# Rows spread by DMA instead of by transposes in a four-layer graph network

## The chip, the cores and the metric

The kernel runs on one core of a Trainium2 chip. The metric is the time of one execution on the device, in microseconds (us); lower is better. A core has five engines with a queue of instructions each: TensorE (PE, matmuls and transposes; its weight loads are listed as PEld), VectorE (DVE), ScalarE (ACT), GpSimd (POOL) and SyncE (SP, which here only issues DMAs). They wait for each other by semaphores.

## The reference

An array x of 32 samples, each 512 nodes by 256 features in float32, goes through four layers; every layer does `x = x + layer(relu(layernorm(x)))`. All layers are attention over the 512 nodes of a sample:

```
layer 0: 4 heads; softmax(q k^T / 8, masked by adj) v, then a product with wo
layer 1: o1 = relu(h mlp1 + b1)
         o2 = elu(gat(o1, no mask, W_fc)) + o1
         o3 = relu(o2 mlp2 + b2)
         relu(elu(gat(o3, adj, W_hand)) + o3)
         gat(o, mask, W): v = o W; e[i,j] = leaky_relu(f1[i] + f2[j]); elu(softmax_j(e) v)
layer 2: 4 heads of 64 features; e[i,j] = leaky_relu(src[i] + dst[j]), masked softmax over j,
         the weighted sum of the heads' features, then elu
layer 3: 8 heads of 32 features; as layer 2 with a prior of adj added to e, then a product with W_out
```

## The kernel before

One sample stays whole in on-chip memory: x as `xt` (128 partitions, 4 groups of nodes, 256 features), everything else in blocks of 128 x 512 floats (62 of them, one tag `block`) and in the eight PSUM banks (tag `bank`). Attention is computed transposed: a block `p[j]` holds 128 source nodes j by 512 target nodes i, so that it is the moving operand of the matmuls `av` directly, and its sum over j is wanted at the end. Softmax is never divided ahead of `av`; the sums of p are inverted and multiplied in afterwards.

The program is not issued in the order in which the source writes it. Every operation is recorded as a `Step` (through `_Recorder`, line 283, which is why all lines of the profile read L283). `Plan.order` then walks through all steps of all 32 samples and puts them in one order for each engine, by planned start and due time; `cost` gives it the assumed times, `STARTS`, `PACE` and `LAYERS` the earliest start of a sample and layer, `URGENT` shifts due times by the name of a tile and the layer, and `PERIOD` spaces the samples. Only the order and the buffers come out of the plan; on the chip the engines wait for semaphores. Two samples and more are in work at any time, so that PE has other samples' matmuls while one sample waits for ACT or DVE. In the steady part the pattern repeats for each two samples.

What the change touches:

- `on_all(name, cols)` (line 742) takes a column per group of nodes (128 x 4) and makes of it one row of 512 that stands on all 128 partitions. It transposes each column, repeated 128 times, on PE into a PSUM bank `pt` and copies that with ACT into a block. It is called four times per sample, in layer 1 only: `r1` in `first_gat` and `r2` in `second_gat` (factors of the target nodes, read by the four p1 or p2 blocks), and `rc` at the end of each `inverse_sums` (the inverse sums, by which `elu2` multiplies what `av` holds).
- `layer2(xt)` (line 914). `separable` computes two banks `av` (features by nodes) and a bank `sm` with the sums. `bars` copies the three to blocks `y3`. Then for each of the four groups of nodes 3 transposes bring them to node-major in a bank `pt`; DVE inverts 4 sums per node (`r4`), multiplies (`ue`), ACT takes the exponential, DVE adds to `xt` in two steps.
- `normalise(avs, sm)` (line 669), used before by layers 0 and 3 only: copies `sm` and `avs` to blocks (`sums`, `raw`), writes four rows of sums to DRAM (`s1`), reads them back spread over 128 partitions (`few`, 128 x 16), inverts them in one short DVE instruction, writes them to DRAM (`s2`) and reads them back repeated over the partitions of each head (`rc`); DVE multiplies (`oT`). All its DMAs are issued by SP.
- SP also loads the samples, stores the results, and spreads the rows `R` of layers 2 and 3 (`rd<-rT`, then 4 or 8 times `R<-rd`, 256 KB each). POOL issues the accumulating DMAs `p<-p`.

Of the kernel before, what the change touches and what calls it, by code (L numbers as in the profile page):

```python
# [15 lines left out]
AF = mybir.ActivationFunctionType  # L16
ALU = mybir.AluOpType
# [3 lines left out]
P = 128  # L21
N = 512
NT = N // P
D = 256
KD = D // P
# [7 lines left out]
H2, F2 = 4, 64  # L33
H3, F3 = 8, 32
# [7 lines left out]

PERIOD = 179.0
STARTS, PACE = (0.0, 0.0, 38.0, 159.0), 85.0
LAYERS = (0.0, 4.0, 2.0, 98.0)

URGENT = {
    "pt:0": 192, "mm:0": 49, "total:0": 70, "av:0": 68, "mm:1": 25, "total:1": -78, "rs1:1": 42, "av:1": -7,  # L50
    "p2:1": 104, "p3:2": -95, "total:2": -542, "ue:2": -396, "mv:3": -121, "mm:3": -158, "p3:3": -723,
    "av:3": -527, "total:3": -695,
}
BLOCKS, KEEP = 62, 2
KEEP_BANKS = 0
# [15 lines left out]
class Plan:  # L71
# [40 lines left out]
    def add(self, attribute, engine, op, args, kw):  # L112
        steps = self.samples[-1]
        out = kw["out"] if "out" in kw else args[0]
        busy, lasts = cost(engine, op, args, kw, out)
        step = self.joined or Step(engine, busy)
        if not step.calls:
# [31 lines left out]
    def release(self, sample, layer):  # L149

        first = len(STARTS) - 1
        return (STARTS[sample] if sample < first else STARTS[first] + (sample - first) * PACE) + LAYERS[layer]

# [165 lines left out]
def cost(engine, op, args, kw, out):  # L319

    src = next((kw[k] for k in ("in_", "in0") if k in kw), args[1] if len(args) > 1 else out)
    if not isinstance(src, bass.AP):
        src = out
    n = 1
    for _, k in (src if op in ("bn_stats", "reduce_max", "tensor_reduce") else out).ap[1:]:
        n *= k
    if engine == "PE":
        return (0.109 if op == "transpose" else max(0.224 if n < 3 else 0.0, n * 0.001676)), 0.165
    pointers = sum(isinstance(kw.get(k), bass.AP) for k in ("bias", "scale"))
    if op == "mul":  # L330
        pointers = 1
    if engine == "ACT":
        busy = 0.05 + 0.000832 * n + 0.093 * pointers + (0.0 if src.tensor.name.startswith(BANKS) else 0.043)
        return busy + (0.093 if "accum_out" in kw else 0.0), 0.12
    if engine == "DVE":
        if op == "reciprocal":
            return 0.06 + 0.0062 * n, 0.085
        if op == "tensor_scalar" and n == N:
            return 0.456, 0.075
        by_pointer = op == "scalar_tensor_tensor" and isinstance(args[2], bass.AP)  # L340
        return 0.066 + 0.00105 * n + (0.06 if by_pointer else 0.0), 0.085
    if engine == "POOL":
        if op == "dma_start":
            return 1.1, (5.2 if n == N else 8.0)
        return (1.0 if n < 16 else 0.683), 0.1
    size = 4
    for _, k in (out.ap if out.tensor.name.startswith(("few", "R", "rc", "x")) else src.ap):
        size *= k
    return 0.4, 3.4 + size / 190e3

# [2 lines left out]
def gnn_stack_kernel(ctx: ExitStack, tc: tile.TileContext, a: dict, out: bass.AP):  # L353
# [13 lines left out]
    x = a["x"]  # L367
# [4 lines left out]
    def T(ap, rearr, **kw):  # L372
        return ap.rearrange(rearr, **kw)
# [17 lines left out]
    ident = const.tile([P, P], F32, name="ident")  # L391
# [20 lines left out]
    r2 = w2[:, :, 3 * H2 + D :]  # L412
# [7 lines left out]
    def new_x():  # L420
        return first.tile([P, NT, D], F32, name="x", bufs=4)
# [4 lines left out]
    with prep_stack, tc.manual_schedule():  # L426

        adj = prep.tile([P, NT, N], I32, name="adj", bufs=1)
        av = T(a["adj"], "(t p) j -> p t j", p=P)
# [6 lines left out]
        row = prep.tile([1, 12 * P], F32, name="row", bufs=1)  # L436
# [146 lines left out]
    def pipelined(stack):  # L583

        big = stack.enter_context(tc.tile_pool(name="big", bufs=1))
        psum = stack.enter_context(tc.tile_pool(name="psum", bufs=8, space=PSUM))
        dram = stack.enter_context(tc.tile_pool(name="dram", bufs=6, space=bass.MemoryType.DRAM))
        q = Plan(nc, PERIOD)
        def block(name):

            return q.tile(big, [P, N], name, BLOCKS, keep=KEEP, tag="block")

        def blocks(name, n):
            return [block(name) for _ in range(n)]

        def bank(name):
            return q.tile(psum, [P, N], name, 8, keep=KEEP_BANKS, tag="bank")

        def small(name, *free):
            return q.tile(big, [P, *free], name, 4)  # L600
# [5 lines left out]
        def col(t):  # L606
            return slice(t * P, (t + 1) * P)
# [61 lines left out]
        def normalise(avs, sm):  # L669


            raws, sums = blocks("raw", len(avs)), block("sums")
            q.scalar.copy(sums, sm)
            for raw, av in zip(raws, avs):
                q.scalar.copy(raw, av)
            s1, s2 = q.tile(dram, [4, N], "s1", 8), q.tile(dram, [4, N], "s2", 8)
            q.sync.dma_start(s1, sums[0:P:32, :])
            few = small("few", 2, 4 * NT)
            c = 4 * N // P
            q.sync.dma_start(few[:, 0, :], T(s1, "h (p c) -> (h p) c", c=c))  # L680
            q.vector.reciprocal(few[:, 1, :], few[:, 0, :])
            q.sync.dma_start(T(s2, "h (p c) -> (h p) c", c=c), few[:, 1, :])
            dst = blocks("oT", len(avs))
            per = 4 // len(avs)
            for i, raw in enumerate(raws):
                rc = block("rc")
                for h in range(per):
                    f = P // per
                    q.sync.dma_start(rc[h * f : (h + 1) * f, :], s2[i * per + h : i * per + h + 1, :].to_broadcast([f, N]))
                q.vector.tensor_tensor(dst[i], raw, rc, op=ALU.mult)  # L690
            return dst
# [49 lines left out]

        def on_all(name, cols):

            pt, b = bank("pt"), block(name)
            for t in range(NT):
                q.tensor.transpose(pt[:, col(t)], cols[:, t : t + 1].to_broadcast([P, P]), ident)
            q.scalar.copy(b, pt)
            return b

        def largest(d):  # L750
# [9 lines left out]
        def inverse_sums(p):  # L760

            total = block("total")
            q.vector.tensor_tensor(total, p[0], p[1], op=ALU.add)
            q.vector.tensor_tensor(total, total, p[2], op=ALU.add)
            q.vector.tensor_tensor(total, total, p[3], op=ALU.add)
            sm, rs = bank("sm"), small("rs1", NT)
            for t in range(NT):
                q.tensor.transpose(sm[:, col(t)], total[:, col(t)], ident)
            q.vector.tensor_reduce(rs, T(sm, "p (t k) -> p t k", k=P), axis=AX.X, op=ALU.add)
            q.vector.reciprocal(rs, rs)  # L770
            rc = on_all("rc", rs)
            q.behind(sm)
            return rc
# [138 lines left out]
                bars(g, avs, sm)  # L912

        def layer2(xt):
            y = blocks("y3", 3)

            def bars(g, avs, sm):
                for b, ps in zip(y, avs + [sm]):
                    q.scalar.copy(b, ps)

            separable(xt, w2, H2, mask1T, bars)
            for t in range(NT):
                pt = bank("pt")
                for k in range(3):
                    q.tensor.transpose(pt[:, col(k)], y[k][:, col(t)], ident)
                r4 = small("r4", H2)
                q.vector.reciprocal(r4, pt[:, D : D + P : F3])
                ue = block("ue")
                u, eu = ue[:, :D], ue[:, D:]
                q.vector.tensor_tensor(  # L930
                    T(u, "p (h f) -> p h f", h=H2), T(pt[:, :D], "p (h f) -> p h f", h=H2),
                    r4[:, :, None].to_broadcast([P, H2, F2]), op=ALU.mult,
                )

                q.scalar.activation(eu, u, AF.Exp)
                q.vector.scalar_tensor_tensor(eu, eu, 1.0, xt[:, t, :], op0=ALU.min, op1=ALU.add)
                q.vector.scalar_tensor_tensor(xt[:, t, :], u, 0.0, eu, op0=ALU.max, op1=ALU.add)

        def layer3(xt):
            oT = []  # L940
# [84 lines left out]
        for i in range(B):  # L1025
            q.begin()
            q.sample, q.left = i, B - i
            xt = q.adopt(new_x() if i else x0, "x", 4)
            if i:
                q.sync.dma_start(xt, xv[i])  # L1030
            for q.layer, layer in enumerate((layer0, layer1, layer2, layer3)):
                layer(xt)
            q.sync.dma_start(ov[i], xt)
# [430 lines left out]
```

## Time and profile before

| | |
|---|---|
| time, median of 3 runs | 3960.52 us (3958.26 to 3962.6) |
| the profiled execution, its own time | 3964.65 us |
| its span in the profile | 3962.9 us |
| granted TensorE clock | 0.992 |
| busy: PE, DVE, ACT, POOL | 98%, 84%, 71%, 14% |
| DMA: bytes, share of the 16 engines | 292.57 MB; SP's queue 14.3%, POOL's 16.1% |

The table's shares are means over the span. In the views that follow, a group of instructions has its engine, the tiles it writes and reads (`out<-in`, buffer numbers left out), its shape and its count; then its busy time and the mean length of one. Matmuls overlap each other, so that a length is not what one costs: the distance from start to start is. A float32 matmul appears as two instructions, a transpose as one. A wait line reads: engine and tile, who released it, the sum in us, how often, the longest. In the timeline the first number is the start in us, the second the length of the group.

### The profile page before, as it was taken

How to read it: one execution, taken by the hardware profiler on the slowest of the kernel's cores; microseconds unless marked ns; L12 is line 12 of the kernel's file. 1: busy time of each engine (PE TensorE's matmuls, PEld its weight loads, DVE VectorE, ACT ScalarE, POOL GpSimd, SP SyncE). 2: the span in 40 equal slices, each digit the busy share in tenths (PEclk: the TensorE clock that was granted, in tenths of full speed). 3: DMA queues.
4: the chain of work that ended last, by engine and by line, in shares of the span. 5: the costliest groups of instructions: out<-in, count | busy, mean ns of one | idle time of the engine just before them, and what ended most of it. 6: DMA issues, size and time to landing. Idle time of an engine off the chain costs nothing.

```text
span 3962.9 us, 52558 instructions
## 1 busy us (share of the span) xinstructions
PE 3890.9 (98%) x17144; PEld 2149.1 (54%) x17144; DVE 3344.2 (84%) x7049; ACT 2805.9 (71%) x5968; POOL 566.4 (14%) x530
## 2 busy tenths in 40 slices
PE   8999999999999999999999999999999999999997
PEld 4655555555555555555555555555555555555552
DVE  6499898888888888988888988888888889888886
ACT  4577677766677766767766777666777667777665
POOL 0001111101111111111101111011111011111010
PEclk8999999999999999999999999999999999999998
DMA  3013333313233223333223333132332233332231
GB/s 101 21 37 81 72 82 84 92 44 92 57 89 92 71 65 76 76 84 84 67 63 78 76 88 88 49 89 59 86 92 73 63 76 76 84 83 69 71 77 50
DMA packets 217616, 292.57 MB, mean 74 GB/s; under 512 B 49915, under 2 KB 103422, under 8 KB 217334
## 3 DMA queue, kind: packets, MB, share of 16 engines
q0 software_dynamic: 68864, 111.18, 16.1%
q1 hardware_dynamic: 148196, 177.69, 14.3%
q8 instruction: 138, 2.26, 0.2%
q14 instruction: 144, 1.18, 0.1%
q10 hardware_dynamic: 274, 0.26, 0.0%
HBM read 158.79 MB, written 19.10 MB: 45 GB/s over the span
## 4 chain that ended last, share of the span: by engine, by line
PE 69%; DVE 17%; DMA 5%; ACT 4%; issue 2%; POOL 2%; SPq 1%; DVEq 0%; ACTq 0%; POOLq 0%
PE mm L283 33%; PE av L283 22%; PE sc L283 5%; PE pt L283 5%; DVE total L283 5%; DVE p L283 5%; DMA R<-rd 4%; PE sm L283 3%; ACT p L283 2%; POOL rs L283 2%; DVE o L283 1%; DVE ue L283 1%; DVE stats L283 1%; DVE x L283 1%; DVE y L283 1%
## 5 line engine op out<-in xcount | busy, mean ns | idle before, releaser
L283 ACT ACTIVATE p<-R,e 128x512 f32<-128x512 f32 x1536 | 993.4, 727 | 53.2 <-DMA R<-rd 52.3
L283 PE MATMUL av<-p,v 128*128 128x512 f32 (+1 forms) x2560 | 930.8, 596 | 4.5 <-DVE p L283 4.4
L283 DVE SCALAR_TENSOR_TENSOR p<-p,e,mask3T 128x512 f32<-128x512 f32 x1024 | 720.5, 749 | 8.1 <-ACT p L283 8.1
L283 POOL TENSOR_TENSOR rs<-ve,mhalf 128x4 f32<-128x4 f32 x128 | 202.5, 1582 | 2755.9 <-DVE ve L283 2634.4
L283 PEld LDWEIGHTS av<-p,v 128*128 128x128 f32 (+1 forms) x2560 | 348.2, 169 | 446.5 <-issue 357.2
L283 DVE TENSOR_TENSOR total<-total,p 128x512 f32<-128x512 f32 x872 | 572.6, 687 | 1.4
L283 PE MATMUL av<-p,vs 128*32 128x512 f32 (+1 forms) x3072 | 504.5, 598 | 5.6 <-DVE p L283 5.4
L283 PE MATMUL mm<-W_fc,o 128*128 128x256 f32 (+1 forms) x2048 | 468.4, 380 | 2.8 <-ACT o L283 2.8
L283 PEld LDWEIGHTS mm<-W_fc,o 128*128 128x128 f32 x2048 | 382.5, 190 | 85.3 <-issue 29.4
L283 POOL DMA_DIRECT2D p<-p x360 | 323.9, 1047 | 564.2 <-PE av L283 191.2
L283 DVE SCALAR_TENSOR_TENSOR p<-p,e,mask1T 128x512 f32<-128x512 f32 x512 | 350.7, 748 | 41.0 <-ACT p L283 40.4
L283 ACT ACTIVATE h<-x,ms,rs 128x256 f32<-128x256 f32 x512 | 280.1, 628 | 122.9 <-DVE ms L283 121.0
L283 DVE TENSOR_TENSOR p<-p,mask0T 128x512 f32<-128x512 f32 x512 | 328.5, 690 | 17.4 <-ACT p L283 17.2
L283 PEld LDWEIGHTS av<-p,vs 128*32 128x32 f32 (+1 forms) x3072 | 138.4, 118 | 342.2 <-issue 238.6
L283 DVE TENSOR_TENSOR total<-p,p 128x512 f32<-128x512 f32 x436 | 288.7, 687 | 0.0
L283 ACT ACTIVATE p<-sc 128x512 f32<-128x512 f32 x512 | 254.3, 679 | 7.8 <-PE sc L283 7.8
L283 PE MATMUL mm<-w,hT 128*128 128x272 f32 (+1 forms) x1024 | 254.4, 393 | 0.9 <-ACT hT L283 0.8
L283 PE MATMUL mm<-hT,mlp_w 128*128 128x512 f32 x512 | 237.6, 596 | 0.0
L283 PE MATMUL mm<-o,mlp_w 128*128 128x512 f32 x512 | 234.7, 596 | 1.3
L283 PE MATMUL sc<-qT,kT 64*128 64x512 f32 x1024 | 230.1, 599 | 0.0
L283 PEld LDWEIGHTS mm<-w,hT 128*128 128x128 f32 x1024 | 190.6, 191 | 61.0 <-issue 15.3
L283 ACT COPY rc<-pt 128x512 f32<-128x512 f32 x64 | 37.4, 585 | 246.8 <-PE pt L283 246.7
(183 smaller groups left out, 5457.5 us busy)
## 6 DMA issues: line engine op xcount, KB each, us to landing
R<-rd SPq DMA_DIRECT2D x384, 256.0 KB
p<-p POOLq DMA_DIRECT2D x360, 256.0 KB, 5.3
x<-in_x_dram SPq DMA_DIRECT2D x32, 512.0 KB
x<-boa POOLq DMA_DIRECT2D x32, 512.0 KB, 5.5
rc<-s SPq DMA_DIRECT2D x128, 128.0 KB
out_dram<-x SPq DMA_DIRECT2D x32, 512.0 KB
rc<-s SPq DMA_DIRECT2D x248, 64.0 KB
s<-sums SPq DMA_DIRECT2D x94, 8.0 KB
```

What stands on the lines that cost most here:

```text
L283: getattr(getattr(self.nc, attribute), op)(*args, **kw)
```

## The change

`on_all` transposes all four columns at once (128 x 4 to 4 x 128), copies the 4 rows to a tile `turned`, lets SP write them to a row in DRAM and lets SP read that row back onto all 128 partitions. `turned` shares its four buffers with `rT` of layers 2 and 3. Layer 2 calls `normalise` ahead of its transposes, so that 2 blocks instead of 3 are transposed, two groups of nodes at a time in one bank, and the elementwise work runs on 512 columns at once from PSUM. The planner's constants are new, and `cost` counts a DMA into r1 and r2 by its destination.

```diff
-PERIOD = 179.0
-STARTS, PACE = (0.0, 0.0, 38.0, 159.0), 85.0
-LAYERS = (0.0, 4.0, 2.0, 98.0)
+PERIOD = 157.0
+STARTS, PACE = (0.0, 7.0, 65.0, 129.0), 95.0
+LAYERS = (0.0, 6.0, 0.0, 143.0)
 
 URGENT = {
-    "pt:0": 192, "mm:0": 49, "total:0": 70, "av:0": 68, "mm:1": 25, "total:1": -78, "rs1:1": 42, "av:1": -7,
-    "p2:1": 104, "p3:2": -95, "total:2": -542, "ue:2": -396, "mv:3": -121, "mm:3": -158, "p3:3": -723,
-    "av:3": -527, "total:3": -695,
+    "stats:0": 39, "mm:0": -259, "p0:0": -88, "oT:0": 727, "mv:1": 15, "pt:1": 831, "mx:1": -151,
+    "nd:1": -62, "r1:1": 187, "total:1": -9, "rc:1": -74, "av:1": -240, "p2:1": -39, "stats:2": -144,
+    "h:2": -284, "p3:2": -269, "av:2": -418, "stats:3": -14, "p3:3": -685, "total:3": -152, "gp:3": 41,
 }
...
-    for _, k in (out.ap if out.tensor.name.startswith(("few", "R", "rc", "x")) else src.ap):
+    for _, k in (out.ap if out.tensor.name.startswith(("few", "R", "r1", "r2", "rc", "x")) else src.ap):
...
         def on_all(name, cols):
 
-            pt, b = bank("pt"), block(name)
-            for t in range(NT):
-                q.tensor.transpose(pt[:, col(t)], cols[:, t : t + 1].to_broadcast([P, P]), ident)
-            q.scalar.copy(b, pt)
+            pt, few = bank("pt"), q.tile(big, [P, P], "turned", 4)
+            q.tensor.transpose(pt[:NT, :P], cols, ident)
+            q.scalar.copy(few[:NT, :], pt[:NT, :P])
+            row = q.tile(dram, [NT, P], "row", 8)
+            q.sync.dma_start(row, few[:NT, :])
+            b = block(name)
+            q.sync.dma_start(b, T(row, "t p -> (t p)")[None, :].to_broadcast([P, N]))
             return b
...
         def layer2(xt):
-            y = blocks("y3", 3)
+            y = []
 
             def bars(g, avs, sm):
-                for b, ps in zip(y, avs + [sm]):
-                    q.scalar.copy(b, ps)
+                y.extend(normalise(avs, sm))
 
             separable(xt, w2, H2, mask1T, bars)
-            for t in range(NT):
+            for t in range(0, NT, 2):
                 pt = bank("pt")
-                for k in range(3):
-                    q.tensor.transpose(pt[:, col(k)], y[k][:, col(t)], ident)
-                r4 = small("r4", H2)
-                q.vector.reciprocal(r4, pt[:, D : D + P : F3])
-                ue = block("ue")
-                u, eu = ue[:, :D], ue[:, D:]
-                q.vector.tensor_tensor(
-                    T(u, "p (h f) -> p h f", h=H2), T(pt[:, :D], "p (h f) -> p h f", h=H2),
-                    r4[:, :, None].to_broadcast([P, H2, F2]), op=ALU.mult,
-                )
-
-                q.scalar.activation(eu, u, AF.Exp)
-                q.vector.scalar_tensor_tensor(eu, eu, 1.0, xt[:, t, :], op0=ALU.min, op1=ALU.add)
-                q.vector.scalar_tensor_tensor(xt[:, t, :], u, 0.0, eu, op0=ALU.max, op1=ALU.add)
+                for i in range(2):
+                    for k in range(KD):
+                        q.tensor.transpose(pt[:, col(2 * i + k)], y[k][:, col(t + i)], ident)
+                u, xs, eu = T(pt, "p (t d) -> p t d", d=D), xt[:, t : t + 2, :], block("eu")
+
+                q.scalar.activation(eu, pt, AF.Exp)
+                eu = T(eu, "p (t d) -> p t d", d=D)
+                q.vector.scalar_tensor_tensor(eu, eu, 1.0, xs, op0=ALU.min, op1=ALU.add)
+                q.vector.scalar_tensor_tensor(xs, u, 0.0, eu, op0=ALU.max, op1=ALU.add)
```

## The prediction

> **What bounds the kernel now.** I read the engine shares on the page first, then the windows view for the stretch without head and tail, then the waits of PE in that stretch. On the page PE is busy for 98% of the span, and its row of tenths is 9 nearly from end to end, while DVE has holes:
>
> ```profile
> PE 3890.9 (98%) x17144; PEld 2149.1 (54%) x17144; DVE 3344.2 (84%) x7049; ACT 2805.9 (71%) x5968; POOL 566.4 (14%) x530
> ...
> PE   8999999999999999999999999999999999999997
> ...
> DVE  6499898888888888988888988888888889888886
> ...
> PE 69%; DVE 17%; DMA 5%; ACT 4%; issue 2%; POOL 2%; SPq 1%; DVEq 0%; ACTq 0%; POOLq 0%
> ```
>
> The windows view splits head, middle and tail (columns: length, busy us and instructions of PE, PEld, DVE, ACT and POOL, granted clock, DMA share, GB/s); the waits of PE in the middle follow:
>
> ```profile
> 0.00:250.00 250.00, 230.09 (x890) 127.14 (x891) 149.36 (x356) 130.40 (x259) 15.43 (x20) 0.95 0.18 50
> 250.00:3750.00 3500.00, 3483.38 (x15372) 1930.92 (x15371) 3031.81 (x6363) 2544.99 (x5438) 535.89 (x494) 1.00 0.32 76
> 3750.00:3963.00 213.00, 177.42 (x885) 91.08 (x883) 163.03 (x332) 130.51 (x274) 15.10 (x16) 0.91 0.24 66
> ```
>
> ```profile
> PE mm L283 <- ACT o L283: 8.4, 17, 1.9
> PE mm L283 <- ACT hT L283: 3.8, 14, 0.3
> PE av L283 <- DVE p L283: 2.8, 3, 1.3
> ```
>
> PE waits visibly for 15 us of 3500, at full clock. So PE is the bound: an instruction taken from PE shortens the kernel by the time until the next may start, and work on DVE, ACT or the DMA queues is free as long as no PE instruction waits for it. Busy time is no proof of this alone (ends of matmuls are modelled), so I also use spacing of starts. In the timeline, twelve transposes run like this, and the small row transposes of layer 1 alike:
>
> ```profile
> 1517.40 0.27 PE L283 MATMUL pt<-ident,mx 128*128 128x128 f32 x1
> 1517.60 1.06 PE L283 MATMUL sm<-p,ones 128*32 128x512 f32 x8
> ...
> 1531.52 1.53 PE L283 MATMUL pt<-ident,y 128*128 128x128 f32 x12
> ...
> 1543.40 0.62 PE L283 MATMUL pt<-ident,rs 128*128 128x128 f32 x4
> ```
>
> (1.53 - 0.27 of the last one's own length - 0.06 of the first's late start) / 11 = 0.11 us from start to start: that is the price of a transpose on PE, not the 0.27 that one lasts. The first pair shows another price: 0.20 us from the transpose to a matmul on 32 columns, so 0.09 us for the change from the full array to columns.
>
> **What the Trainium skill says.** "TensorE: Matmul & The Clock Gate", Part 4, gives about 275 ns for a 128x128 transpose inside a kernel; the trace agrees for the length (273 ns median), but in a burst only 109 ns of it stand on PE. "TensorEngine Tiling (Array Packing)", Key Properties, says that changing the tiling mode drains TensorE; the 0.09 us agree. "DMA: Bandwidth & Descriptors", Anatomy of one DMA, gives a fixed cost of about 2 us, mostly the receipt of the write, and says that semaphores are waited for on the issuing sequencer ahead of dispatch. The trace agrees: SP issues the read of a small row only once its write has landed, 1.83 us later:
>
> ```profile
> 1608.69 0.62 SPq L283 DMA_DIRECT2D rd<-rT  x1
> 1610.52 2.60 SPq L283 DMA_DIRECT2D R<-rd  x4
> ```
>
> **The change part by part.**
>
> *Work on PE.* on_all is called 4 times per sample (r1, rc, r2, rc): 4 transposes of 128x128 become one with 4 output rows. Layer 2 transposes 8 instead of 12 times per sample. Over 32 samples 512 + 384 = 896 go and 128 + 256 = 384 come, 512 fewer x 0.109 = 55.8 us. The narrow transpose has no row here; the nearest, of 16 columns (es), also takes 0.11 us to the next start; between 0.06 and 0.20 us each, 128 of them would move the sum by -6 to +12. The diff's new constants of the planner also reorder PE. In the order of the built programs the tiling mode changes 558 times before and 491 times after (the branch that isn't run counts alike in both): 67 x 0.093 = 6.2 us. Together 62 us of PE.
>
> *ACT.* Gone: 128 copies of r and rc (38.3 + 37.4 us) and 128 exps of ue (45.4). New: 128 copies of 4x128 (about 0.25 each, the rT row: 32) and 64 exps of 128x512 (about 0.63: 40). The 96 copies of y3 become 96 of raw and sums. 49 us less.
> *DVE.* Gone: r4, the product ue and its two additions (15.7 + 45.6 + 51.0 + 50.3 = 163 us). New: 64 products oT (0.69), 128 additions of 128x512 (0.69), 32 reciprocals few (0.24): 140. 23 us less. Neither is on the path, and both get lighter; I count nothing. The cover is PE's own work.
>
> *DMAs.* 128 x (one row written, one 256 KB broadcast), and for layer 2 32 x (3 small ones and 4 of 128 KB): 480 more issues on SP, at 0.3 to 0.65 us about 0.2 ms of its 3.9 ms, and 50 MB on 292.57 (+17%). The share of the DMA engines rises from 0.32 to about 0.37. SP's queue is in order: behind a row waiting for its transpose or its landing stand other samples' R loads, sums and rows; ACT (p) and DVE (oT) wait for these, and PE for p and oT.
>
> *The new latency.* A row used to take 4 transposes and a copy, about 1.3 us. Now: transpose 0.27, copy 0.25, write 1.83, broadcast 3 to 7 us (256 KB of p<-p lands in 5.3 by the page; I take 5.3), so 7.7. For r1 the DVE op follows (0.55): 8.2 to the first p. For r2 exp and mask (0.72 + 0.75): 9.1. For rc the chain of elu2 (0.69 + 3 x 0.65 + 2 x 0.69 = 4.0): 11.7 until o2. For layer 2 (sums 0.59, three hops of 1.8 to 2, reciprocal 0.24, issues 1.7, landing 2 to 5, product 0.69): 11 to 14. What must be weighed against this is how much PE work the order puts between. I added up the PE instructions of the built order with the spacings of the trace (0.43 us for 512 columns, 0.22 for 256, 0.11 for a transpose):
>
> r1 to the first av: 3.0 us before, 16.7 to 17.0 after. r2 to the first av: 3.0 and 9.4 before, 17.2 and 12.1 after (even and odd samples). rc to the first matmul on o2: 8.2 and 16.7 before, 18.8 and 17.5 after. Layer 2's sums to its transposes: 0.1 to 1.0 before, 19.9 after.
>
> So the new planner constants moved every consumer back further than the latency grew; 3 us remain at the tightest place (odd r2), 6 or more elsewhere. In the middle I take 0, between -14 (before, PE loses 0.9 us each second sample where layer 2's sm waits for DVE's total; this may go) and +25 (a broadcast lands 5 us late behind a burst of R loads in one of six rows, less than a quarter of it uncovered, plus waits at odd r2).
>
> *Head and tail.* The head's order differs a little (release times); I take its time as before. In the tail the cover is thinner: for sample 30 layer 2's sums have 5.6 us of PE work instead of the 11 needed, for sample 31 rc has 9.3 against about 11.7, and layer 2's first transposes follow layer 1's last without filler (3.5 us before). I take +6, between 0 and +15.
>
> *Sum.* 62 - 6 = 56 us less. The profiled execution took 3964.65 us (span 3962.9), 4.1 above the median of 3960.52. 3964.65 - 56 = 3908.7, on the scale of the median 3904.6: **3904**.
>
> **Rivals.**
> 1. *The broadcasts collide.* The DMAs come in bursts (4 or 8 R loads of 256 KB, then p<-p). For it: in the contended stretch at 1504.9 ACT waits 0.8 and then 1.7 us for R issued over 5 us earlier. Against: 12 to 20 us of cover. If PE loses 1.5 us per sample, 48 us, 3904 + 32 to 48 = 3936 to 3952. Chance 0.10.
> 2. *SP's queue becomes the pace* (slower). 160 new round trips block SP for about 2 us each, and a late one holds the next sample's, so cover is lost in chain. It decides once PE loses more than (56 + 8) / 160 = 0.4 us per round trip; at 0.7 us the time is 3904 + 112 = 4016, at 0.5 us 3984. For it: SP order of the changed program weaves rows of two samples with sums and R loads. Against: SP is idle before most issues now and what it waits for is mostly producers (945 us for rT in the queue's own waits). Chance 0.08.
> 3. *PE's saving is taken up by DVE*, at 0.87 of the middle, so that the transposes' place turns into waits for p or total: time between 3953 and 3968, no change. Against: DVE gets 23 us less. Chance 0.04.
> That the transposes do not go is excluded by the built order.
>
> **How the numbers follow.** Likeliest case 0.78, own range 3878 to 3938 (3904 with the bounds above: -14 middle, -6 tail, -6 narrow transposes, to +25 middle and +9 tail). Rivals 0.10, 0.08, 0.04. A measurement can tell 0.2% from no change, 8 us here: faster 0.88, same 0.04, slower 0.08. The range 3872 to 3942 takes in half of rival 1; out of it are rivals 2 and 3, the rest of 1 and a few hundredths below.
>
> **What would show it.** Right: about 16600 PE instructions, the rows pt<-ident,ew and pt<-ident,rs with 4 columns x64 each; PE still 97% or more and 0.99 in the middle; middle waits of PE under 40 us; total waits of SP changed, without effect. A longer tail by 5 to 10 us. Wrong: PE waits for p behind DMA r<-row, or for o behind DMA rc<-row, over 60 us in all; PE in the middle at 97% or less.

## The result and the profile after

The change made the kernel slower: 4030.45 us (median of 4 runs, 4027.66 to 4036.13) against 3959.39 for the kernel before on the same chip, a ratio of 1.0176 with a 95% interval of 1.0164 to 1.0189. That is 70 us more, where 56 less were predicted. The profiled execution took 4027.66 us, its span is 4025.9, so the profile stands 3 us under the median.

The same lines of the page as before (engines: busy us, share of the span, instructions; then PE's row of tenths and the shares of the chain that ended last):

```profile
PE 3845.7 (96%) x16632; PEld 2095.4 (52%) x16632; DVE 3323.7 (83%) x6761; ACT 2738.1 (68%) x5904; POOL 532.1 (13%) x530
...
PE   7999999999999999999999999999999999999977
...
PE 71%; ACT 11%; DMA 7%; DVE 6%; issue 2%; SPq 2%; POOL 0%; DVEq 0%; ACTq 0%; POOLq 0%
```

PE has its 512 instructions less. It is busy for 45 us less, and yet the span is 63 us longer: PE stands still (is not busy) for 4025.9 - 3845.7 = 180 us, against 3962.9 - 3890.9 = 72 before. The windows view says where (columns as before: length, busy us of PE, PEld, DVE, ACT, POOL, granted clock, DMA share, GB/s):

```profile
0.00:250.00 250.00, 228.72 (x852) 131.30 (x854) 128.81 (x319) 124.25 (x258) 15.54 (x21) 0.99 0.22 59
250.00:3750.00 3500.00, 3393.12 (x14753) 1849.97 (x14749) 2995.63 (x6054) 2455.55 (x5312) 497.75 (x491) 0.99 0.37 88
3750.00:4026.00 276.00, 223.90 (x1031) 114.16 (x1030) 199.31 (x390) 158.34 (x337) 18.78 (x18) 0.89 0.25 70
```

The head is nearly the old one (PE stands for 21 us, 20 before). In the middle PE stands for 107 us instead of 17, in the tail for 52 instead of 36. The largest waits of PE in the middle (us in total, times, longest):

```profile
PE mm L283 <- DVE oT L283: 42.9, 25, 2.6
PE pt L283 <- ACT h L283: 23.5, 25, 2.9
PE mm L283 <- ACT hT L283: 21.2, 42, 0.9
```

None of them is directly a wait for what the change gave a longer way. PE does not wait for p behind r or for o behind rc, and for layer 2's oT at its transposes only 5.5 us. It waits for oT, the normalised blocks of layers 0 and 3, whose code the change does not touch, and for h and hT, the layer norm at a layer's start. Before, these rows had 0, 0 and 3.8 us in the middle.

One such wait in full. The timeline of SP's queue shows the inverse sums of layer 0 for the second sample of a pair (start, us, tiles, how many). The rows s<-few at 1547.06 and rc<-s at 1549.68 belong to the chain ahead of it, layer 2's sums of another sample, and the rows with `row` to layer 1:

```profile
1545.62 0.52 SPq L283 DMA_DIRECT2D s<-sums  x1
1547.06 0.31 SPq L283 DMA_DIRECT2D s<-few  x1
1547.46 0.41 SPq L283 DMA_DIRECT2D few<-s  x1
1549.68 2.71 SPq L283 DMA_DIRECT2D rc<-s  x4
1554.18 0.33 SPq L283 DMA_DIRECT2D s<-few  x1
1555.54 0.47 SPq L283 DMA_DIRECT2D row<-turned  x1
1559.88 1.99 SPq L283 DMA_DIRECT2D rc<-s  x3
1562.06 1.93 SPq L283 DMA_DIRECT2D rc<-row  x1
1564.04 1.20 SPq L283 DMA_DIRECT2D rc<-s  x1
```

The chain that ended last and DVE's timeline continue it:

```profile
1562.12 1.86 SPq L283
1563.99 0.05 issue
1564.04 5.75 DMA rc<-s
```

```profile
1565.96 0.69 DVE L283 TENSOR_TENSOR oT<-raw,rc 128x512 f32<-128x512 f32 x1 [2.52 <-DMA p<-p]
1569.88 0.69 DVE L283 TENSOR_TENSOR oT<-raw,rc 128x512 f32<-128x512 f32 x1 [2.51 <-DMA rc<-s]
```

The sums leave at 1545.62 and the second product ends at 1570.57: 25 us. Three of the four broadcasts go out at 1559.88; the fourth stands in the queue behind layer 1's `rc<-row` and lands 5.75 us after its issue. PE has done all that stood between by 1568.1 and waits until 1570.6.

I followed every such chain of the middle in this way, from the issue of s<-sums to the end of the last product, by the order of instructions on SP and DVE. For layer 0 the two samples of a pair take 18.9 and 27.3 us before, and 19.7 and 24.3 after. So the chain is not longer on the whole. What changed is what it is set against: the PE work that the built order puts between sums and product was 19.1 and 35.2 us before, enough for both, and is 20.2 and 22.3 after, 2 us too little for the second. These waits are about half of the 42.9 us: the lines of the middle put 21.0 us to layer 0's matmuls (mm<-woT,oT) and 21.8 to layer 3's (mm<-L_WoT,oT).

### The profile page after: what moved, and what is told of

The parts are those of the page before. It is cut to its first block, busy times and chain, and to the rows that moved or that the text cites. A ratio compares the mean times of both kernels' runs of the same rounds, so it can differ in the third digit from the quotient of the medians.

```text
span 4025.9 us, 52303 instructions
## 1 busy us (share of the span) xinstructions
PE 3845.7 (96%) x16632; PEld 2095.4 (52%) x16632; DVE 3323.7 (83%) x6761; ACT 2738.1 (68%) x5904; POOL 532.1 (13%) x530
## 4 chain that ended last, share of the span: by engine, by line
PE 71%; ACT 11%; DMA 7%; DVE 6%; issue 2%; SPq 2%; POOL 0%; DVEq 0%; ACTq 0%; POOLq 0%
PE mm L283 40%; PE av L283 21%; ACT p L283 4%; DMA rc<-s 4%; PE pt L283 4%; PE sm L283 3%; PE sc L283 3%; DVE p L283 2%; ACT e L283 2%; ACT h L283 2%; SPq L283 2%; DMA s<-few 1%; DVE total L283 1%; DMA R<-rd 1%; ACT hT L283 1%
## 5 line engine op out<-in xcount | busy, mean ns | idle before, releaser
L283 DVE SCALAR_TENSOR_TENSOR p<-p,e,mask1T 128x512 f32<-128x512 f32 x512 | 363.0, 744 | 75.0 <-ACT p L283 73.3
L283 POOL TENSOR_TENSOR rs<-ve,mhalf 128x4 f32<-128x4 f32 x128 | 170.8, 1335 | 1908.1 <-DVE ve L283 1901.7
L283 PE MATMUL mm<-o,mlp_w 128*128 128x512 f32 x512 | 250.1, 611 | 2.0 <-DVE o L283 2.0
L283 ACT ACTIVATE e<-y 128x512 f32<-128x512 f32 x192 | 117.0, 625 | 188.2 <-DVE y L283 187.9
L283 ACT COPY v<-mm 128x512 f32<-128x512 f32 (+2 forms) x384 | 161.2, 444 | 116.0 <-PE mm L283 83.6
L283 ACT COPY raw<-av 128x512 f32<-128x512 f32 x190 | 109.2, 583 | 188.4 <-PE av L283 186.0
```

Source lines behind the costliest of these rows:

```text
L283: getattr(getattr(self.nc, attribute), op)(*args, **kw)
```

## The experiments

A ratio has a half-width (of its 95% interval) of about 0.0017 here, 7 us, so a difference of two runs is known to about 9 us; differences below are of ratios times 3960. The work of PE that an edit adds or removes is counted as in the prediction (0.109 us per transpose, 0.093 per change of tiling mode).

**Constants and code apart (four runs).** The diff changes code and the planner's constants (`PERIOD`, `STARTS`, `PACE`, `LAYERS`, `URGENT`) at once. e_ac_bc is the changed code with the old constants, e_bc_ac the old code with the new ones; e_onall_ac and e_l2_ac are the new constants with one half of the new code each.

```diff
 # e_ac_bc: code of after, constants of before;  e_bc_ac: the reverse
-PERIOD = 157.0
-STARTS, PACE = (0.0, 7.0, 65.0, 129.0), 95.0
-LAYERS = (0.0, 6.0, 0.0, 143.0)
+PERIOD = 179.0
+STARTS, PACE = (0.0, 0.0, 38.0, 159.0), 85.0
+LAYERS = (0.0, 4.0, 2.0, 98.0)
 ...
```

> The changed code (on_all by DMA, layer 2 by normalise) planned with the constants of the kernel before (PERIOD, STARTS, PACE, LAYERS, URGENT). Theory A, order: the new constants, which put two samples close together and leave more of both samples for the end, cost the time, and the code saves PE work as forecast: 3900 to 3940. Theory B, transfers: the new round trips make PE's operands late whatever the order: 4000 or more, as the old constants were made for short rows.

> The code of the kernel before, planned with the new constants. Theory A, order: it shows the new ramp, the new tail (39 us longer from the last transpose of a maximum to the end) and pairs of samples 64 and 13 us apart: 4010 to 4060, no faster than the changed kernel. Theory B, transfers: without the new DMAs the steady part loses its waits for oT: 3960 to 3985.

> Only on_all is changed (layer 2 as before), new constants. Theory A: 42 us of PE less than the old code under these constants, so about 40 below e_bc_ac. Theory B: 128 of the 160 new round trips are in it, so it is near the changed kernel, 4010 to 4040, and above e_bc_ac.

> Only layer 2 is changed (on_all by transposes as before), new constants. Theory A: 14 us of PE less than the old code, about 10 to 15 below e_bc_ac. Theory B: a fifth of the new round trips, so 3970 to 3990, between the old code under these constants and the changed kernel.

Measured: 4368.16 (ratio 1.1035, 1.1017 to 1.1053), 4318.26 (1.0904, 1.0885 to 1.0922), 4297.97 (1.0844, 1.0826 to 1.0862) and 4311.69 (1.0887, 1.0869 to 1.0905). All four are over 300 us slower than before, far more than was expected of any of them. So constants and code fit each other or don't, and the constants alone, with the code kept, move this kernel by 8 to 9% (4368.16 against 4030.45 for the changed code, 4318.26 against about 3962 for the old). An edit that changes the list of operations cannot be tried on this kernel without either keeping the order or fitting it anew; the other runs do the one or the other.

**Layer 1's rows within the changed order (e_pe, e_spare).** Both keep the order and plan of the changed kernel. In e_pe a row is made by four transposes and a copy again, and its DMAs are not issued. In e_spare they are issued at their old places, with the broadcast going into a tile in DRAM that nobody reads; so its queue and bytes are those of the change, its destination is not.

```diff
+            turn, copy, write, read = q.samples[-1][-4:]
+            turn.calls = [
+                ("tensor", "transpose", (pt[:, col(t)], cols[:, t : t + 1].to_broadcast([P, P]), ident), {}) for t in range(NT)
+            ]
+            copy.calls = [("scalar", "copy", (b, pt), {})]
+            write.calls, read.calls = [], []                # e_pe
             ...
+            write.calls = [("sync", "dma_start", (row, b[:NT, :P]), {})]        # e_spare
+            read.calls = [("sync", "dma_start", (spare, T(row, "t p -> (t p)")[None, :].to_broadcast([P, N])), {})]
```

> The changed kernel with its order and plan kept, only that layer 1's rows are made as before: four 128x128 transposes and one ACT copy straight into the block; the two DMAs of a row are not issued. PE gets 384 transposes more (3 of 0.109 us for each of 128 rows, 42 us). Theory A: the order stays and PE has 42 us more, so 4065 to 4080. Theory B: 42 us more of transposes, but the waits for oT go (30 to 40 us of wait and as much again at half rate behind it): 3965 to 4010, with PE's waits for DVE oT under 20 us.

> As e_pe (rows by four transposes and a copy, +42 us of PE), but the same two DMAs of each row are still issued at the same places of SyncE's queue: the row goes to DRAM and its broadcast of 256 KB goes into a spare DRAM tile that nobody reads. Nothing waits for the rows any more, but queue and DMA traffic are those of the change. Theory A: as e_pe, 4065 to 4080. Theory B: queue and traffic make oT late as in the changed kernel, so about 4070 as well, while e_pe lies 60 us or more below it. If e_pe and e_spare are both near 3990, what costs time is the wait of layer 1's own chain for its rows.

Measured: 4035.76 (1.0183, 1.0166 to 1.0200) and 4062.92 (1.0254, 1.0237 to 1.0271). PE's wait for oT in the middle, changed kernel 42.9 us, e_pe, then e_spare:

```profile
PE mm L283 <- DVE oT L283: 13.2, 19, 1.9
```

```profile
PE mm L283 <- DVE oT L283: 28.1, 26, 1.9
```

The second sample's layer-0 chain took 22.8 us in e_pe and 23.8 in e_spare, against 24.3. e_pe does 42 us more on PE than the changed kernel and is 3 us slower, so without the transfers the same work takes 39 us less. e_spare brings 28 of them back although nobody waits for its rows; the 11 that remain, little more than the error, are left for the wait for the rows. Neither theory had this: A expected e_pe at 4065 or more, B the whole loss in the transfers and e_pe at 4010 or less. It is about half: the transfers cost nearly what the transposes saved, PE's wait for layer 0's and layer 3's oT goes with them, and e_pe still stands 73 us above before.

**The place in the queue alone (e_pull).** SP's later broadcasts of a block are issued right behind its first, so that no `rc<-row` stands between as at 1562.

```diff
-        steps, at = self.order(), {}
+        steps, at = gathered(self, self.order()), {}
         ...
+        # gathered: on SP, outside layer 1, a later rc<-s moves up to the first one of its block
```

> The changed kernel, its order kept on every engine but SyncE: there the later rc<-s broadcast of a block is issued directly behind the block's first one, so that no broadcast rc<-row of layer 1 stands between the two in SyncE's queue. Theory A (the order that was written for the change sets the time: samples nearly in step with each other, a longer tail; SyncE's queue takes no part): within 8 us of the changed kernel, 4030. Theory B (the new row transfers on SyncE make layer 0's and layer 3's inverse sums late, PE waits for oT, and runs at half rate after each wait): PE's wait for DVE oT falls from 55 us to under 25, and with what follows each wait the time is 3960 to 3995. If only the transfers' landing is late and not the issue of the fourth broadcast, B also gives about 4025.

Measured: 4030.68 (1.0169, 1.0151 to 1.0186), no change. PE's wait for oT in the middle fell from 42.9 to 31.5 us, all of it layer 0's, whose chain is 1 us shorter (23.3), but the wait for h behind it rose from 23.5 to 31.8.

```profile
PE mm L283 <- DVE oT L283: 31.5, 25, 2.3
```

So the fourth broadcast's place, which the timeline shows so plainly, was worth nothing by itself, and an oT wait that goes is not time saved as long as another chain stands close behind.

**Layer 2's trip within the changed order (e_nol2, e_l2spare, e_none).** After the runs with fitted orders below, the trip of layer 2's sums was open. Again in the changed kernel's order: e_nol2 does not issue its seven transfers per sample and leaves out layer 2's division by the sums (the products take a constant), e_l2spare does the same but issues the transfers, with few<-s and rc<-s landing in spare DRAM tiles, and e_none is e_nol2 with e_pe's rows, so without any of the new transfers.

```diff
                 q.vector.tensor_tensor(dst[i], raw, rc, op=ALU.mult)
+                if q.layer == 2:
+                    q.samples[-1][-1].calls = [
+                        ("vector", "tensor_tensor", (dst[i], raw, eps[:, 0:1].to_broadcast([P, N])), dict(op=ALU.mult))
+                    ]
+            if q.layer == 2:
+                for step in q.samples[-1][-12:]:
+                    if step.engine == "SP":
+                        step.calls = []          # e_l2spare: few<-s and rc<-s go to spare DRAM tiles
 ...
```

> The changed kernel, its order and plan kept, but layer 2's seven transfers per sample are not issued: sums, inverse sums and their four broadcasts stay out, the reciprocal takes a constant, and both products of raw and rc take a constant in place of rc. That leaves layer 2's normalisation out. PE has the changed kernel's work, and layer 2's products wait for the raw blocks alone. If layer 2's trip through DRAM is what makes the changed code slow in every order so far (4000 to 4030) while layer 1's half alone went to 3936: 3960 to 3990. If its cost lies in the order and in what DVE and PE do, 4015 to 4030.

> As e_nol2, but the seven transfers are issued at their places of SyncE's queue and land in spare DRAM tiles that nobody reads; the products still take a constant. Traffic and queue are those of the change, the waits for the inverse sums are gone. If layer 2's cost is traffic and queue (layer 0's and layer 3's trips late behind it), within 10 us of the changed kernel, 4020 to 4040; if it is the wait for layer 2's own inverse sums, within 10 us of e_nol2.

> Both halves' transfers gone: the changed kernel's order, rows by four transposes and a copy (42 us more of PE), and layer 2 as in e_nol2, its normalisation left out. PE has then 20 us less than before the change. If the transfers together are the whole cost, 3940 to 3960; what it stands above that is the price of the order alone, which gives a longer tail and brings pairs of samples nearly into step: 3990 to 4010 if the order costs some 50 us by itself.

Measured: 4005.89 (1.0107, 1.0091 to 1.0124), 4026.36 (1.0169, 1.0152 to 1.0185) and 4011.98 (1.0125, 1.0108 to 1.0142). PE's wait for oT in the middle, e_nol2 and then e_l2spare:

```profile
PE mm L283 <- DVE oT L283: 27.5, 23, 2.2
```

```profile
PE mm L283 <- DVE oT L283: 47.9, 29, 2.7
```

Layer 0's second chain took 22.9 and 24.2 us. Layer 2's trip costs 27 us, about 25 of them by traffic and queue; the wait for its own result is within the error (3 us). The two halves add up: with both gone (e_none, 42 us more on PE) the same work takes 62 us less, against 39 + 27 = 66 one by one. So the new transfers take back, to within the error, the whole 62 us that PE was relieved of. With none of them (e_none) layer 0's second chain is 21.4 us, 2.9 shorter and below its cover of 22.3. PE's wait for oT in the middle is then

```profile
PE mm L283 <- DVE oT L283: 11.3, 13, 2.0
```

and all of it is layer 3's. The two traces show most of the 62: with the transfers PE stands for 180 us instead of 137 (41 of the 43 in the middle, 32 of them for layers 0 and 3's oT), and half clock adds 40 us to its busy time instead of 30 (last section); that is 53.

e_none is left with the order. PE has 20 us less to do than before the change (128 transposes and the 67 mode changes), no new transfer is there, and it is 50 us slower than before: the order costs 70. Strictly that is the order with layer 2's new element work on ACT and DVE, which e_none keeps; the two were not parted. Its windows:

```profile
0.00:250.00 250.00, 229.06 (x857) 132.73 (x857) 125.36 (x314) 123.41 (x252) 15.55 (x21) 0.98 0.20 52
250.00:3750.00 3500.00, 3433.97 (x15185) 1897.15 (x15185) 3016.21 (x6096) 2507.05 (x5355) 500.19 (x493) 1.00 0.32 75
3750.00:4012.00 262.00, 211.97 (x976) 107.69 (x974) 182.24 (x353) 146.68 (x300) 14.84 (x16) 0.88 0.22 63
```

In the middle PE stands for 66 us (17 before), mostly for hT (21.2) and h (18.9), the layer norms, which have too little other work beside them in this order. In the tail it stands for 50 us (36 before), and at a lower clock.

**Fitted orders (five runs).** The code stays, and the planner's constants are searched anew. e_order2 is the changed code with a first such set. The other four come from one kind of search, in which SP's transfers and POOL's power instruction count as slower: r_after is the changed code, r_before the code before, r_onall has layer 1's half of the change alone, r_l2 layer 2's half alone.

```diff
 # r_onall: code of before with the new on_all, and
-PERIOD = 179.0
-STARTS, PACE = (0.0, 0.0, 38.0, 159.0), 85.0
-LAYERS = (0.0, 4.0, 2.0, 98.0)
+PERIOD = 164
+STARTS, PACE = (0, 24, 125, 192), 105
+LAYERS = (0, 46, 151, 125)
 ...
```

> The changed code with another set of the planner's constants (start times of samples and layers, priorities by tile and layer), found by a longer search; every instruction is that of the changed kernel, only the order of issue differs. Theory A: the change's code is worth its 62 us of PE where the order suits it: 3900 to 3960. Theory B: the row transfers cost in any order: 4000 to 4060.

> The changed code once more in another order: the planner's constants found by a search that takes the transfers of SyncE and the power instruction of GpSimd as slower than the planner's own figures, so that more work lies between the sums of layers 0 and 3 and the products that need them. Every instruction is that of the changed kernel. If the excess over before is made of waits for oT and h (55 and 48 us in the changed kernel, 29 and 55 us in the other order) and of half clock behind them, this order should take most of that away: 3910 to 3960. If the row transfers and layer 2's round trips cost in any order, it stays at 3990 or above, as the other order did.

> The code before the change, with constants found by the same search, under the same durations and for the same time. It tells what the change is worth when each code has an order of its own from the same source. If PE's 62 us count in full, it lies 50 to 65 us above the run of the changed code of this call; if longer chains and traffic of the change eat them, within 15 us of it or below. Against the kernel before itself: 3930 to 3970, since there the middle has only some 15 us of waits to win.

> Layer 1's half of the change alone (rows by one transpose and two DMAs of SyncE; layer 2 as before), with constants searched for this code in the same way as for the two kernels of the last call (before's code so ordered: 3961; the whole change: 4005). PE has 384 transposes of 0.109 us less than before, 42 us. If the row transfers are what costs (their traffic and queue 27 us and the wait for rows 10 us, from the two kernels with PE-made rows), the saving is eaten: 3945 to 3975. If they fall free once the order suits: 3915 to 3935. If this half carries the whole loss of the change: 3990 or more.

> Layer 2's half alone (its sums inverted through DRAM and both blocks normalised ahead of the transposes; layer 1's rows by four transposes as before), with constants searched for this code in the same way; the search came less far here. PE has 128 transposes less, 14 us, and some 6 us less of changes of tiling mode. If this half's third round trip per sample is what costs: 3980 to 4010, near the whole change. If it is harmless: 3940 to 3955. A value over 4010 would say the order that the search found is poor, and tell nothing of the half.

| kernel | us | ratio, 95% interval |
|---|---|---|
| e_order2 (whole change) | 3999.66 | 1.0097, 1.0081 to 1.0114 |
| r_after (whole change) | 4005.31 | 1.0114, 1.0097 to 1.0130 |
| r_before (no change) | 3961.41 | 1.0000, 0.9991 to 1.0009 |
| r_onall (layer 1's half) | 3935.60 | 0.9937, 0.9920 to 0.9953 |
| r_l2 (layer 2's half) | 4028.56 | 1.0167, 1.0150 to 1.0184 |

r_onall is faster than both kernels, by 25 us (19 to 32) against the one before. Its windows of middle and tail:

```profile
250.00:3750.00 3500.00, 3477.75 (x15347) 1933.40 (x15348) 3088.02 (x6497) 2513.25 (x5509) 528.01 (x507) 1.00 0.36 86
3750.00:3932.00 182.00, 136.34 (x626) 64.60 (x625) 119.96 (x238) 101.96 (x220) 3.02 (x3) 0.86 0.16 52
```

PE is at full clock and stands for 22 us of the middle, nearly as little as before, with a DMA share almost that of the changed kernel (0.36 and 0.37). So the row transfers can be covered, and a saving is left: 25 us, where 42 of transposes were priced. How much of it is the transposes is not exact, as the order is another one too; r_before, from the same kind of search, gained nothing. For the whole change two other orders (e_order2 and r_after) gained 31 and 25 us on the first and stayed 38 and 45 above before. r_l2 tells nothing of its half, as its expectation allowed: PE waits there for layer 1's exponentials, which that half does not touch,

```profile
PE pt L283 <- DVE ew L283: 43.7, 14, 4.1
```

and that is a poor order. Whether the whole change has an order as good as r_onall's was not found out.

## Why the prediction was wrong

*Work on PE: right.* 512 transposes went, and the counts are those predicted (16632 instructions). The narrow transpose, which had no row before, takes 0.11 us to the next start:

```profile
1554.95 0.27 PE L283 MATMUL pt<-ident,rs 128*4 128x128 f32 x1
1555.06 3.60 PE L283 MATMUL av<-p,v 128*128 128x512 f32 x8
```

All but two of the 128 do so. Without what half clock adds (19 us before, 40 after), PE's busy time fell by 66 us, where 62 were predicted.

*ACT and DVE: off the path, as said.* DVE's busy time fell by 20.5 us (predicted 23); ACT's by 67.7, where 49 were predicted.

*The new latency: covered, as said, though two terms were too small.* The hop through DRAM was priced at 1.83 us from a quiet place (the Trainium skill's 2 us beside it, "DMA: Bandwidth & Descriptors", Anatomy of one DMA, are fitted for transfers issued from GpSimd, and these are SP's); in the changed kernel the row's read is issued 4.0 us after its write in the median of 128, and 8.0 at most (6.5 in the timeline above, 1555.54 to 1562.06). Layer 2's chain takes 17.9 and 19.9 us for the two samples of a pair, where 11 to 14 were priced; it found 19.9 us of cover. No large row of PE's waits names p behind a new row, o behind rc or layer 2's transposes, and the runs give 11 and 3 us for the waits on the new results, about what the error is. PE's work between producer and consumer was the right measure for the chains to which it was put.

*"In the middle I take 0, between -14 and +25": the step that failed.* PE's idle time there rose by 90 us. Two things were left out of it.

First, cover and latency were weighed for the four new chains alone. What stands behind them in SP's queue and shares the DMA engines was only priced as a total: 480 issues, 0.2 ms of SP's 3.9, and a share of 0.32 that becomes 0.37. But layer 0 sends its own sums through that queue, the new order cut its cover from 35.2 to 22.3 us, and the transfers made the chain 2.9 us longer (21.4 without them, 24.3 with), past it; layer 3's matmuls wait 21.8 us for their oT with the transfers and 11.3 without. The prediction had named what stands behind the new transfers ("other samples' R loads, sums and rows", DVE for oT) and did not go on to count it. The runs give 28 + 25 us for traffic and queue, and 62 with the waits for the new results. They do not part the queue's order from the sharing of the DMA engines; e_pull speaks only against the place of one broadcast.

Second, the new order was credited with what it did for the new chains and charged with nothing. It costs 70 us without any of the transfers (e_none, with layer 2's new element work): layer norms uncovered in the middle, and the tail.

*Tail "+6, between 0 and +15": too small.* PE stands for 16 us longer there, at a granted clock of 0.89 over 276 us instead of 0.91 over 213; in e_none, where no transfer takes part, it is 14 us longer at 0.88. So the tail comes with the order, not from layer 2's late sums.

*The sum.* By the runs -62 of work, +62 of transfers and +70 of order give the +70; this closes by construction, as the last two are differences of runs. The two traces give a sum of their own: 66 us less work of PE at full clock, 108 more in which it stands, 21 more of half clock, together the 63 by which the span grew. Rival 2 had the right sign and nearly the right place: it said SP's queue decides from 0.4 us per round trip, and 62 us over 160 are 0.39, whether by the queue or, as in rival 1, by the shared engines. What put the time beyond 4000 was the order, which no rival had. Of what was to show the forecast wrong, "PE in the middle at 97% or less" came (3393 of 3500), while the waits named for it did not: the harm went to other chains.

## What to carry to other kernels

A transfer that is itself covered can still cost what it saves: list every chain that uses the same queue, and give each the sum of cover against latency, the untouched ones first. Where an order is fitted to a program, price the new order for all its chains, or keep it fixed and switch single transfers off and into spare tiles; those two runs part traffic from waiting. And halves of a change are worth trying with an order of their own: here one half was the gain.

## What the runs showed of the hardware

PE's clock halves after waits shorter than I thought. Two waits of the changed kernel for oT, from PE's timeline:

```profile
1570.63 4.54 PE L283 MATMUL mm<-woT,oT 128*128 128x256 f32 x12 [2.51 <-DVE oT L283]
...
2053.51 2.86 PE L283 MATMUL mm<-woT,oT 128*128 128x256 f32 x12 [1.98 <-DVE oT L283]
```

The same twelve matmul instructions take 1.7 us longer after the first. The windows view around it (granted clock third from the end):

```profile
1560.00:1571.00 11.00, 8.49 (x23) 3.95 (x22) 5.97 (x14) 0.55 (x2) 1.72 (x2) 1.00 0.77 172
1571.00:1574.40 3.40, 3.40 (x10) 2.69 (x9) 3.40 (x10) 3.13 (x6) 0.47 (x1) 0.51 0.02 5
1574.40:1580.00 5.60, 5.36 (x37) 2.18 (x36) 5.60 (x12) 5.60 (x12) 2.13 (x1) 1.00 0.00 1
```

The clock is half for 3.4 us and full again. The Trainium skill, "TensorE: Matmul & The Clock Gate", Part 1, What's actually happening, describes a free-running activity window of about 3.4 us and half clock after an idle one. Length and grid agree: all stretches at half clock in the clock records of the changed kernel start a whole number of 3.413 us apart. But here a window need not be idle throughout. Nine stretches of the middle follow a window of this grid in which PE stood for 1.8 to 2.6 us in all and worked for the rest. In this trace every window with more than 2.0 us was followed by half clock, none at full clock with 1.78 or less was, and between them it went both ways. It is no sharp rule: in e_nol2 a window with 1.5 us was followed by half clock too. The two waits above fit: a boundary of the grid, at 2052.2, divides the wait of 1.98 us, which cost nothing more, while the wait of 2.51 us lies within one window. So a wait of 2.5 us cost 4.2 here.

The clock records have ten such stretches in the middle, against none before. Counting only what PE worked in them, half clock adds 40 us to its busy time in the whole changed kernel and 19 before, so some 20 of the 70 us are lost in this way.
